# Layer 0 of a four-layer convolution stack: loads written into the expansion, last product with two pixel rows as column tiles

## The chip, the core and the metric

The kernel runs on one core of a Trainium2 chip. TensorE (PE) multiplies matrices out of SBUF into PSUM, VectorE (DVE) and ScalarE (ACT) work on SBUF and PSUM, GpSimd (POOL) and SyncE (SP) mostly issue DMAs here. The metric is the time of one execution on the device in microseconds (us), lower is better; of several runs the median is taken.

## The reference

The input x has 4 images of 64 channels and 256 x 256 pixels. Four layers follow each other, each of the form x = x + conv(group_norm(x)). Only the first matters here:

```python
def _L0_conv_ref(x, w_in, w_dw, fft_filter, w_out):          # hidden = 192, c2 = 384
    x = jnp.einsum('bchw,oc->bohw', x, w_in)                 # 64 -> 384 channels
    # 8 x 8 patches: filter each patch in the frequency domain
    xf = jnp.fft.rfft2(xp) * fft_filter
    xp = jnp.fft.irfft2(xf, s=(8, 8))
    # depthwise 3 x 3 convolution over the whole image
    x = lax.conv_general_dilated(x, w_dw, (1, 1), [(1, 1), (1, 1)], feature_group_count=384)
    x1, x2 = jnp.split(x, 2, axis=1)
    x = jax.nn.gelu(x1, approximate=False) * x2
    return jnp.einsum('bchw,oc->bohw', x, w_out)             # 192 -> 64 channels

x = x + _L0_conv_ref(_gn(x), ...)                            # 32 groups of 2 channels
```

The three layers behind it (a 3 x 3 convolution, a masked one, and a Fourier layer) are not touched.

## The kernel before

All arithmetic is in float32. Layer 0 treats the filter in a patch and the 3 x 3 convolution as one linear map from the 64 pixels of a patch (and its neighbours to the right and below) to 64 pixels, with matrices for each of the 384 channels that are made once at the start (`tables`, `weights`) and kept in DRAM (`wts`).

An image has 32 rows of 32 patches. Eleven rows form a block, three blocks an image, twelve blocks in all (`blocks`; p counts them, i0 is the first patch row, -1, 10 or 21). A block is worked in four quarters (kb) of 48 of the 192 channel pairs. A quarter has two stages:

- The expansion (`expand`, lines 444 and 450 on PE): for each of up to 12 patch rows t, the normalized input is multiplied by `w_in` into PSUM, with pixels on partitions. Even t take 32 PE instructions of 128 columns of weights, odd t 64 of 64 columns. ACT and DVE each copy half of the result into the tile u (line 459 for even t, lines 461 to 463 for odd t). Two rows t are in PSUM at once.
- The convolutions (`convolve`, lines 494 and 503 on PE), g = 0 to 11: four channel pairs each. ACT takes the GELU (line 510), DVE multiplies (line 511), and POOL stores the tile h to the DRAM tensor g of the block (line 514). The weights w come from `wts` by SP (line 471), one load for two g.

The last product of layer 0, 192 to 64 channels by `w_out`, needs all four quarters of a block. So it runs one block late: block p - 1 is projected while block p is worked, in 16 units, one after each of the convolutions g = 1, 4, 7 and 10. A unit (`project`) covers one pixel row r of the patches (8 of them) and four of the eight pixel columns (half 0 or 1). Its g loads (`load_g`, lines 546 and 550) and the x rows for the residual (`load_r`, line 559) come by SP. Of the 192 channels 128 are multiplied with `wo1` (line 591), 64 with `wo6` (line 598). The two column tiles of PE are the left and the right half of the image row (s). A unit works on two banks of PSUM, and each instruction covers the valid patch rows only: 11 rows give 176 columns, 10 rows 160. The DVE adds the product to the residual tile r (lines 607, 610, 612); after the second half it takes bn_stats of r for the next layer's norm (line 618), and POOL stores r (line 622). The units of the last block run alone at the end.

The loop also loads x for the next image's statistics (`load_stats`, line 627, summed by DVE in line 320) and, in the fourth quarter, the rows of the next block (`load_x`, line 418, normalized by ACT in line 256).

The order on PE, DVE, ACT and SP is the order of the program, written by hand; only POOL's is left to the framework. An engine waits for nothing but semaphores: buffers that come free, and data. So SP works off its DMA list as fast as buffers allow. PSUM is four pairs of banks, taken in turn. The rings of SBUF buffers are `l0x` 4 (x and statistics), `l0w` 4, `l0h` 4, and 2 each for the g loads and r.

## Time and profile before

| | us |
|---|---|
| median of 3 runs | 6649.44 |
| lowest, highest | 6638.31, 6666.61 |
| profiled execution | 6626.21 |
| its span in the profile | 6624.4 |
| mean granted PE clock in it | 0.953 |
| first projection unit, last one (start) | 432.0, 4060.1 |

The numbers of the prediction come from the one profiled execution. Busy times of the engines overlap; what counts is which of them the others wait for in each stage. In a group's line the last part is the idle time of the engine just before these instructions, and what ended it: "<-ACT u L459" is a wait for ACT's line 459, "issue" a stop for which the profile shows no wait. PEld is the weight load of PE. A float32 matmul of the program is two instructions on PE.

### The profile page before, as it was taken

How to read it: one execution, taken by the hardware profiler on the slowest of the kernel's cores; microseconds unless marked ns; L12 is line 12 of the kernel's file. 1: busy time of each engine (PE TensorE's matmuls, PEld its weight loads, DVE VectorE, ACT ScalarE, POOL GpSimd, SP SyncE). 2: the span in 40 equal slices, each digit the busy share in tenths (PEclk: the TensorE clock that was granted, in tenths of full speed). 3: DMA queues.
4: the chain of work that ended last, by engine and by line, in shares of the span. 5: the costliest groups of instructions: out<-in, count | busy, mean ns of one | idle time of the engine just before them, and what ended most of it. 6: DMA issues, size and time to landing. Idle time of an engine off the chain costs nothing.

```text
span 6624.4 us, 238282 instructions
## 1 busy us (share of the span) xinstructions
PE 6040.5 (91%) x106712; PEld 3213.7 (49%) x106712; DVE 4275.7 (65%) x5924; ACT 3238.8 (49%) x4564; POOL 1050.4 (16%) x1646
## 2 busy tenths in 40 slices
PE   2999999999999999999999986999899999999987
PEld 1455555555555555555555543333344444443576
DVE  5556555555555555555555545999798898885355
ACT  4454434344434444344444422777777887783211
POOL 3111111111111111111111111111022222221011
PEclk9999999999999999999999997999999999999855
DMA  8577777777878877877767669999666666677889
GB/s 236 152 206 211 216 213 222 218 216 213 230 213 238 219 222 207 223 214 220 210 193 206 188 194 247 232 229 228 165 177 176 168 180 173 173 187 264 318 351 394
DMA packets 878510, 1447.67 MB, mean 219 GB/s; under 512 B 77252, under 2 KB 586452, under 8 KB 875444
## 3 DMA queue, kind: packets, MB, share of 16 engines
q1 hardware_dynamic: 725284, 923.09, 54.8%
q0 software_dynamic: 148672, 500.14, 21.7%
q8 instruction: 843, 13.81, 0.9%
q10 hardware_dynamic: 3536, 9.20, 0.5%
q14 instruction: 175, 1.43, 0.1%
HBM read 932.08 MB, written 500.04 MB: 216 GB/s over the span
## 4 chain that ended last, share of the span: by engine, by line
PE 82%; DMA 6%; ACT 5%; DVE 3%; issue 3%; SPq 0%; POOL 0%; ACTq 0%; DVEq 0%; POOLq 0%
PE pc L503 18%; PE pc L494 12%; PE m L869 10%; PE psu L444 9%; PE one L1110 8%; PE div L1069 6%; PE po L591 4%; ACT u L459 4%; PE psu L450 4%; PE psz L1099 2%; PE po L598 2%; DMA x<-x 2%; PE psa L1297 2%; DMA g<-g 2%; PE psy L1444 1%
## 5 line engine op out<-in xcount | busy, mean ns | idle before, releaser
L511 DVE TENSOR_TENSOR h<-h,pc 128x374 f32<-128x374 f32 x1152 | 574.7, 541 | 1268.7 <-ACT h L510 1267.7
L510 ACT ACTIVATE h<-pc 128x374 f32<-128x374 f32 x1152 | 492.6, 480 | 1824.9 <-PE pc L503 1822.0
L503 PE MATMUL pc<-u,w 64*16 64x374 f32 (+2 forms) x27648 | 1244.1, 483 | 0.0
L494 PE MATMUL pc<-u,w 64*64 64x374 f32 x9216 | 928.6, 494 | 81.1 <-DVE u L463 32.2
L514 POOL DMA_DIRECT2D g<-h x576 | 416.7, 723 | 3111.0 <-DVE h L511 2904.7
L503 PEld LDWEIGHTS pc<-u,w 64*16 64x16 f32 (+2 forms) x27648 | 413.8, 92 | 769.5 <-issue 768.9
L444 PE MATMUL psu<-win,xn 64*128 64x96 f32 x8704 | 627.0, 283 | 131.8 <-ACT u L459 110.5
L459 DVE COPY u<-psu 64x384 f32<-64x384 f32 x1088 | 604.3, 555 | 167.7 <-PE psu L444 155.7
L459 ACT COPY u<-psu 64x384 f32<-64x384 f32 x1088 | 560.0, 515 | 238.9 <-PE psu L444 218.8
L444 PEld LDWEIGHTS psu<-win,xn 64*128 64x128 f32 x8704 | 574.0, 192 | 202.6 <-ACT u L459 143.6
L1055 DVE TENSOR_TENSOR q<-xn 128x2313 f32<-128x2313 f32 (+2 forms) x256 | 627.4, 2492 | 1.7 <-ACT xn L256 1.7
L1110 PE MATMUL one<-z,wp 32*32 32x512 f32 x16384 | 592.1, 596 | 17.8 <-issue 13.6
L494 PEld LDWEIGHTS pc<-u,w 64*64 64x64 f32 x9216 | 350.3, 133 | 531.0 <-issue 354.7
L256 ACT ACTIVATE xn<-x,nb,r 128x1024 f32<-128x1024 f32 (+3 forms) x272 | 486.8, 1793 | 244.6 <-DMA x<-x 140.8
L1056 ACT ACTIVATE q<-q 128x2313 f32<-128x2313 f32 (+2 forms) x256 | 529.0, 2086 | 32.7 <-DVE q L1055 31.2
L450 PE MATMUL psu<-win,xn 64*64 64x96 f32 x17408 | 458.2, 252 | 81.9 <-issue 57.2
L1069 PE MATMUL div<-q,ones 64*32 64x512 f32 x8192 | 466.3, 594 | 12.9 <-ACT q L1056 9.3
L1110 PEld LDWEIGHTS one<-z,wp 32*32 32x32 f32 x16384 | 367.6, 103 | 223.6 <-issue 80.1
L450 PEld LDWEIGHTS psu<-win,xn 64*64 64x64 f32 x17408 | 395.5, 137 | 126.0 <-issue 77.0
L1143 POOL DMA_DIRECT2D x<-r x512 | 275.5, 547 | 969.8 <-DVE r L1140 945.1
L591 PE MATMUL po<-g,wo 128*64 128x176 f32 (+1 forms) x3072 | 315.8, 348 | 63.3 <-DMA g<-g 41.3
L869 PE MATMUL m<-t,wk 64*64 64x512 f32 x3072 | 341.1, 588 | 0.0
(162 smaller groups left out, 6668.1 us busy)
## 6 DMA issues: line engine op xcount, KB each, us to landing
g<-h POOLq DMA_DIRECT2D x576, 374.0 KB, 7.0
x<-x SPq DMA_DIRECT2D x240, 640.0 KB, 6.4
w<-wt SPq DMA_DIRECT2D x288, 448.0 KB, 8.4
x<-x SPq DMA_DIRECT2D x100, 1024.0 KB, 14.2
g<-g SPq DMA_DIRECT2D x414, 187.0 KB, 5.7
g<-g SPq DMA_DIRECT2D x736, 93.5 KB, 6.0
x<-in_x_dram SPq DMA_DIRECT2D x256, 256.0 KB, 8.1
x<-o POOLq DMA_DIRECT2D x128, 512.0 KB, 8.2
```

Source lines behind the costliest of these rows:

```text
L444: nc.tensor.matmul(ps[s][:, k, at], xn[halves[s], n : n + 2].rearrange("p n r w -> p (n r w)"), win[halves[s], kb, 0 : 2 * PB], start=True ...
L450: nc.tensor.matmul(ps[s][halves[1 - odd], k, at], xn[halves[s], n + odd].rearrange("p r w -> p (r w)"), win[halves[s], kb, PB * (1 - odd) ...
L459: copy(at(h, 8 * s + o), v[k, c : c + PB])
L494: nc.tensor.matmul(out(C * c, C, k, h), w[halves[h], k, 2 * (G % 2) + c, 0:C], cells(h, 4 * g + 2 * k + c, 0, 0), start=True, stop=False, ...
L503: nc.tensor.matmul(out(q, m, k, h), w[halves[h], k, 2 * (G % 2) + c, c0 : c0 + m], cells(h, 4 * g + 2 * k + c, down, right), start=False, ...
L511: nc.vector.tensor_mul(h[:, k], h[:, k], ps[k][:, 1, 0:L])
L591: nc.tensor.matmul(out(k, s, x), wo1, moving(g1[:, 2 * k], 2 * half + k, s, x), start=(x == 0), stop=False, skip_group_check=True,)
L869: nc.tensor.matmul(rows2(m)[halves[j], s], w[dx][halves[s]], ts[n][halves[s], i, 2 * j : 2 * j + 2, dx : dx + W], start=(dx == 0), stop=(d ...
L1055: nc.vector.tensor_sub(d, p0, p1)
L1056: nc.scalar.activation(d, d, AF.Square)
L1069: ins = nc.tensor.matmul(ps[quarters[j], h], ones[halves[h]], q[n, g, k][halves[h], r + 2 * j : r + 2 * j + 2, o : o + W], start=(m == 0), ...
L1110: ins = nc.tensor.matmul(rows2(ps[g])[quarters[j], k], w[quarters[i]], z[quarters[i], h, 2 * j + dy : 2 * j + dy + 2, dx : dx + W], tile_p ...
```

## The change

- A unit now covers two pixel rows and two of the eight pixel columns: n // 4 gives the pair of rows, n % 4 the pair of columns. The two column tiles of PE are the two pixel rows. Each instruction takes all 374 columns of a plane as it lies in memory, halo and invalid rows too, so a unit has 8 matmuls of 374 columns instead of 16 of up to 176. DVE then picks the valid elements out of PSUM with two adds of 352 elements (four where the two rows have different limits).
- The residual tile holds two pixel rows at full width, in two buffers as before: loads and stores of r move runs of 1 KB, where they moved 512 bytes.
- The channels are assigned anew to `wo1` and `wo6`, and a unit's g loads are four DMAs (some split in two), by 96, 32, 64 and 64 partitions, in runs of 2 x 374 and 374 elements.
- The weights in DRAM lie so that a w load has one run of 3584 bytes on each partition, where it had two of 1792.
- The units stand after g = 0, 3, 6 and 9. The g loads of the units after g = 0 and 3 follow their unit at once; those of the units after 6 and 9 are kept in the list `later` and stand in the next expansion behind t = 7 and t = 9. The r load stands behind g = 1, for a block's first quarter in the expansion. Loads of x (statistics or next rows) stand in the expansion behind t = 9, 10 and 11, the others as before.
- The statistics of r are a list `tasks` of six bn_stats chunks for a row pair, filled by the fourth unit of a quarter (g = 9); two are taken after each convolution that has no unit, one behind each t of an expansion.
- The rings `l0x`, `l0w` and `l0h` have 3 buffers instead of 4, and the w load looks two ahead instead of three.

The diff, cut to its core:

```diff
-        p_xn, p_x = pool("l0xn", NR + 1), pool("l0x", 4)
-        p_w, p_h = pool("l0w", 4), pool("l0h", 4)
+        p_xn, p_x = pool("l0xn", NR + 1), pool("l0x", 3)
+        p_w, p_h = pool("l0w", 3), pool("l0h", 3)
...
-        wts = [dr.tile([2, 64, 2, Q, NC], F32, name=f"wt{t}") for t in range(HID // C)]
+        wts = [dr.tile([2, 64, Q, 2, NC], F32, name=f"wt{t}") for t in range(HID // C)]
...
+        def load_g(p, n):
+            if not (0 <= p < NB and n < 16):
+                return
+            rr, q0 = (2 * (n // 4), 2 * (n // 4) + 1), 2 * (n % 4)
...
+            g1 = pools[0].tile([128, 2, 2 * L], F32, tag="g1", name=f"g1_{p}_{n}")
+            g6 = pools[1].tile([128, 2, L], F32, tag="g6", name=f"g6_{p}_{n}")
+            loads[p, n] = g1, g6
+            parts = [(g1[Q:128], 1, slice(0, HID // 2), q0, 2), (g1[0:Q], 0, slice(C, HID // 2), q0, 2)]
+            parts += [(g6[halves[q]], 0, slice(0, C), q0 + q, 1) for q in range(2)]
...
+        def split(lo, hi):
+            out = [(k, min(2, hi - k)) for k in range(lo, hi, 2)]
+            if len(out) < (NR + 1) // 2:
+                out[-1:] = [(hi - 2, 1), (hi - 1, 1)]
+            return out
...
+            for q in range(2):
+                for s in range(2):
+                    nc.tensor.matmul(
+                        po[halves[s], q, 0:L], wo1, g1[:, s, q * L : (q + 1) * L],
+                        start=True, stop=False, skip_group_check=True,
+                    )
+            for q in range(2):
+                for s in range(2):
+                    nc.tensor.matmul(
+                        po[halves[s], q, 0:L], wo6[halves[q]], g6[halves[q], s],
+                        start=False, stop=True, tile_position=(q * C, s * C), skip_group_check=True,
+                    )
...
+                    o = rt[h, lo:hi].rearrange("p i (j x w) -> p w i x j", x=2, w=P)[:, (q0 + q + 1) % P]
+                    nc.vector.tensor_add(o, o, v)
...
+            def stats(at, chunks):
+                for h, (i, m) in chunks:
+                    nc.vector.bn_stats(bst[h, at, :], rt[h, i : i + m].rearrange("p i w -> p (i w)"))
+            chunks = zip(*([(h, c) for c in split(lo, hi)] for h, lo, hi in groups))
+            tasks.extend((stats, next(slot), c) for c in chunks)
...
+        def task(n=1):
+            for _ in range(min(n, len(tasks))):
+                f, *args = tasks.pop(0)
+                f(*args)
...
                     for t in range(NR + 1):
                         if 0 <= i0 + t < NP:
                             expand(p, kb, t)
+                        task()
+                        if t in (7, 9) and later:
+                            load_g(*later.pop(0))
+                        if t == 7 and kb == 0:
+                            load_r(p - 1, 0)
+                        if t >= 9:
+                            if kb == 3 and t - 9 < len(fresh):
+                                load_x(fresh[t - 9])
+                            elif kb < 3 and nk:
+                                loaded.append(nk.pop(0))
+                                load_stats(b + 1, loaded[-1])
                     for g in range(NG):
                         G = NG * kb + g
                         if g % 2 == 0:
-                            load_w(p * (HID // 8) + G // 2 + 3)
+                            load_w(p * (HID // 8) + G // 2 + 2)
                         convolve(p, kb, g)
                         if g < NG - 1:
                             self.next_norms()
-                        if g in (1, 4, 7, 10):
-                            unit()
+                        if g in (0, 3, 6, 9):
+                            unit(wait=g > 3)
+                        else:
+                            task(2)
+                        if g == 1 and kb < 3:
+                            load_r(p - 1, kb + 1)
```

## The prediction

> **What bounds the kernel now.** I read the page first, then a table of four stretches of one quarter block of layer 0, then the groups of instructions inside layer 0's blocks, then two stretches of the timeline. The page gives the engine shares and the DMA by slices:

> ```profile
> span 6624.4 us, 238282 instructions
> PE 6040.5 (91%) x106712; PEld 3213.7 (49%) x106712; DVE 4275.7 (65%) x5924; ACT 3238.8 (49%) x4564; POOL 1050.4 (16%) x1646
> DMA  8577777777878877877767669999666666677889
> ```

> TensorE (PE) is busy nine tenths of the span, and the change touches only layer 0 (slices 3 to 25, about 390 to 4062 us). DMA at 0.7 to 0.8 there is an average over two very different stages. The table by stretches shows them for one expansion (1121 to 1147) and the convolutions after it (columns: busy us of each engine, granted clock, DMA share, GB/s):

> ```profile
> 1121.00:1135.00 14.00, 11.72 (x312) 10.72 (x305) 10.85 (x21) 10.02 (x20) 0.96 (x2) 1.00 1.04 299
> 1135.00:1147.00 12.00, 8.59 (x248) 7.71 (x240) 9.35 (x18) 8.73 (x18) 0.00 (x0) 1.00 0.08 16
> 1150.00:1200.00 50.00, 50.00 (x880) 21.23 (x882) 24.66 (x41) 9.41 (x22) 10.42 (x14) 1.00 0.87 249
> ```

> In the convolutions PE never stops and VectorE (DVE) works half the time. In the expansion PE has gaps, DVE works almost all the time, and the DMA is full for 14 us and then idle for 12. The groups say why PE stops in the expansions of all blocks (390 to 3940 us; the last part is PE's idle time and what ended it):

> ```profile
> L444 PE MATMUL psu<-win,xn 64*128 64x96 f32 x8064 | 578.7, 282 | 123.1 <-ACT u L459 101.8 <-issue 18.7 <-ACT u L462 2.0
> L450 PE MATMUL psu<-win,xn 64*64 64x96 f32 x15872 | 418.0, 252 | 57.5 <-issue 57.2
> ```

> So 102 us go to copies out of PSUM, and 18.7 + 57.2 = 75.9 us to "issue", where no wait explains the stop. Around these stops the instruction queue's 16 KB fetches are in flight and come late, so I take them for late instructions. The timeline of an undisturbed expansion shows the copy loop:

> ```profile
> 3701.93 2.03 PE L444 MATMUL psu<-win,xn 64*128 64x96 f32 x32
> 3702.57 1.00 DVE L511 TENSOR_TENSOR h<-h,pc 128x374 f32<-128x374 f32 x2 [0.55 <-ACT h L510]
> 3704.03 2.26 DVE L459 COPY u<-psu 64x384 f32<-64x384 f32 x4 [0.47 <-PE psu L444]
> 3706.24 2.20 PE L444 MATMUL psu<-win,xn 64*128 64x96 f32 x32 [0.80 <-ACT u L459]
> 3708.47 2.26 DVE L459 COPY u<-psu 64x384 f32<-64x384 f32 x4 [0.45 <-PE psu L444]
> 3709.31 2.19 SPq L559 DMA_DIRECT2D r<-in_x_dram  x2
> ```

> Even rows' copies (2.26 us on DVE) free the PSUM pair, PE then needs 2.2 us for the next even row, and only then can DVE go on: a ring of 4.44 us for two rows (3704.03 to 3708.47). DVE idles 0.45 us in each turn, but a delay of DVE larger than that is never made good. The last line matters too: SP issues an r load at 3709 that stands in the program behind a convolution and a unit beginning after 3728. SP runs ahead of PE as far as buffers allow.

> **The projection units (PE).** A unit now is 12 steps: 16 wo1 matmul instructions two at a time, 16 of wo6 four at a time, 176 columns each:

> ```profile
> 1011.43 1.60 PE L591 MATMUL po<-g,wo 128*64 128x176 f32 x16
> 1012.95 0.92 PE L598 MATMUL po<-g,wo 64*64 64x176 f32 x16
> 1013.68 0.50 PE L494 MATMUL pc<-u,w 64*64 64x374 f32 x2
> ```

> That is 1013.68 − 1011.43 = 2.25 us; with ten patch rows (160 columns) about 2.05. The new unit has half the instructions, always 374 columns: 4 + 2 = 6 steps. A convolution has 10 steps of 374 columns (16 instructions four at a time, 48 eight at a time) in 3.52 us, 0.352 a step with its switches, so 6 × 0.352 = 2.11 us. Ends: 6 × 0.31 = 1.86 (spacing of the steps of L494 alone), or 2.25 / 2 × 374 / 176 = 2.39 if time goes strictly by column. I take 2.11, whose row has these very columns. Of the 176 units beside convolutions 114 have eleven rows, 62 ten: 114 × 0.14 − 62 × 0.06 = 12 us saved (56 saved to 37 lost).

> **Statistics moved into DVE's ring.** The residual adds stay 352 elements for each pixel column, and lie beside convolutions, where DVE has half its time free: nothing, as before. The bn_stats are as many as before (six chunks a row pair, 0.64 us each at 512 elements, 0.40 at 256), but leave their place. Their row in the view of that line (shortest, median, longest ns):

> ```profile
> L618 DVE BATCH_NORM_STATS2 bst<-r x288: 404/676/699, 448.4 to 4064.2; 128x6 f32<-128x512 f32 x96, 128x6 f32<-128x384 f32 x32, 128x6 f32<-128x256 f32 x16
> ```

> Two of 512 in a row take 1.28 us in the timeline, hence 0.64. Before, three follow a unit inside the convolutions. Now six are queued at g = 9 and drain two at g = 10 (free), two behind the last convolution, one behind expansion row 0, one behind row 1. Waiting behind them on DVE are the copies, and behind those PE. With X the start of the expansion: DVE ends the last products at X + 1.64 (3703.57). Even first row, before: copies of row 2 begin at 3708.47, X + 6.54. After: 1.64 + 1.28 = 2.92; copies 2.26, 5.18; a chunk 0.64, 5.82; odd copies 1.70, 7.52; a short chunk 0.40, 7.92. Delay 1.38. By the same steps: both late chunks short (ten-row blocks), 1.14; odd first row, where three chunks stand ahead of the first copies, 5.66 against 3.75 (1042.75 to 1046.50 in the timeline), 1.91; seven expansions behind a pair whose two rows have unequal limits, where every chunk is two instructions, 3.46. Twelve each of the first three: 16.6 + 13.7 + 22.9 + 7 × 3.46 = 77 us on the path. Ends: 0, if PE would be stopped there by late instructions anyway, and 43 × 2.6 = 112, if nothing of it finds a gap. I take 77, from the undisturbed rows.

> **The loads.** Writing two of four g loads of a quarter and three image loads into expansion rows 7 to 11 moves them in SP's program, not in time: their buffers are free from g = 7 to 9 on, and the last thing SP waits for ahead of them is the w load of g = 10. So they go out about 9 us ahead of the expansion (only in a block's first quarter do they wait for the last g store). That is 2 × 1.15 + 3 × 0.52 = 3.9 MB, with stores and w some 5.5 MB, 18 to 22 us at 249 to 299 GB/s: the DMA is full until about X + 12, where it now is until X + 14. The r load, which now runs ahead into the expansion, no longer does, as it stands behind a g load that waits for its unit. Instruction stops: in the timelines some 13 of the 75.9 us lie in the first 8 us of expansions, where DVE will be late anyway, and 45 past 14 us, some 18 of these in second and third quarters, where the DMA will be quiet sooner. I take 13 + 9 = 22 saved, ends 76 saved and 40 lost. [...]

> **Shallower rings.** h, 4 to 3: from ACT's start to landing 1.8 + 7.1 (median of the blocks; longest 10.7), 12.5 at worst; three convolutions and a unit are 12.7: nothing, though little is left. w, 4 to 3: the load at g = 4 stands behind unit 1's g load, which waits for PE; 4 × 3.52 + 2.1 − 4.1 of issue = 12.1 us are left for a landing of 8.6 (longest 13.3; the 4.1 are SP's for a unit's g loads from 1016.22 on). x, 4 to 3: ScalarE's normalization has 11 us for 8.1 to 11.5, and some 2 us of slack behind it. I put 3 us (0 to 25).

> **The tail** (3937 to 4062, last block's units alone) is bound by DMA, share 1.04 to 1.07. r moves 5.8 of its 29 MB, now in 1 KB runs where there were 512 B, and half of it before the first g store has landed. Against that stand four adds and twelve statistics for the last, unequal pair, some 6 us. Net 6 saved (15 saved to 6 lost). [...]

> **Sum.** −12 + 77 − 22 + 3 − 6 = +40 us. The profiled execution took 6626.2 us (span 6624.4), below the median of three by 23; 6626.2 + 40 = 6666, and on the median 6649.4 + 40 = 6689. Its own range is +5 to +80.

> **Rivals.** (1) Stalls overlap: PE stops for DVE instead of for instructions, and the 77 swallow the 76. Then −12 + 1 − 6 + 3: about −14, no change. For it: both are about 1.75 us an expansion; against it: most stops lie late, past the first two rows. (2) Faster: the DMA is quiet through all expansions, the 75.9 us vanish, the steps cost 1.86, and half of DVE's delay finds gaps: −56 − 76 + 38 − 6 = −100; with the steps at 2.11, −56. It needs SP's burst not to come, and decides once the stops fall under some 20 us. (3) Slower still: w is late. If its landing behind a g load passes 12.1 us, PE waits at g = 8 in each quarter: 1.5 us × 44 = 66, together +106; the longest landings now (13.3) are past that point. (4) The wide units are no cheaper (2.39) with all else as forecast: +89.

> **Numbers.** Forecast 0.5, rival 1 0.2, rival 2 0.12, rivals 3 and 4 together 0.18. About 0.5% (33 us) is what a measurement can tell from no change. Of the forecast's half, 0.31 lies above +33; with 0.18, slower is 0.49. Faster: 0.12 and 0.03 of rival 1, 0.15. Same: 0.36. The range goes from −50 (6600) to +115 (6765); the likeliest case alone has 6654 to 6729.

> **What would show it.** Right: units of 2.1 us; two bn_stats of r behind the last product and one each between the first copies, with the even copies of row 2 at X + 7.9; expansions longer by 1 to 2 us, the idle time of L444 ended by DVE copies up by some 70; SP's g issues ahead of X. Wrong: no bn_stats ahead of the copies, issue stops in the expansions at zero or above 100 us, PE waiting for w or h.

## The result, and the profile after

The changed kernel takes 6832.19 us (median of 4 runs, 6830.44 to 6843.61), the kernel before 6643.88 us in the same comparison (6630.05 to 6666.61). The ratio is 1.028, with a 95% interval of 1.0254 to 1.0306: slower by 2.8%, some 186 us. The forecast was +40 us with a range that ended at +115; the sign was right, the size was not, and the time lies above the range.

The page of the changed kernel, the lines that were shown of before:

```profile
span 6828.7 us, 230801 instructions
PE 6112.8 (90%) x103640; PEld 3120.7 (46%) x103640; DVE 4339.7 (64%) x6132; ACT 3242.0 (47%) x4564; POOL 975.4 (14%) x1550
DMA  8476778677878786867676769999956667667889
```

PE executes 3072 instructions fewer and is busy 72 us longer (6112.8 against 6040.5), at a mean granted clock of 0.936 in place of 0.953. The groups of PE inside layer 0's blocks (390 to 4270 us) say where:

```profile
L445 PE MATMUL psu<-win,xn 64*128 64x96 f32 x8064 | 616.0, 294 | 160.1 <-ACT u L460 101.3 <-DVE u L460 31.8 <-issue 23.6
L451 PE MATMUL psu<-win,xn 64*64 64x96 f32 x15872 | 458.3, 264 | 104.8 <-issue 75.5 <-ACT u L464 18.4 <-DVE u L464 6.4
L495 PE MATMUL pc<-u,w 64*64 64x374 f32 x8496 | 861.3, 495 | 107.6 <-DVE u L460 27.8 <-DVE u L464 27.5 <-DMA w<-wt 27.0
```

These are the same expansion instructions as L444 and L450 before, in the same number. Before, they were busy 578.7 + 418.0 = 996.7 us and had 123.1 + 57.5 = 180.6 us of idle time ahead of them; now 1074.3 and 264.9. That is +78 us of busy time and +84 us of waiting, +162 us together. Stops taken for late instructions ("issue") went from 75.9 to 99.1, where 22 us less were forecast. Waits for w (27.0 us) are new in the convolutions; the view of before has none.

The whole difference of the spans, 204 us, by stages (sums over PE's stretches in the two traces): expansions +162, of which 121 in the blocks' first quarters (291.5 to 412.1); convolutions +44; units beside them −21; from the last convolution to the last product of layer 0 −14 (124.2 to 110.3); the first block +8; from the last product to the end of the program +26; the start −1.

The table by stretches shows a typical expansion, the one that the prediction showed for before (block 3, second quarter), and the convolutions behind it:

```profile
1183.70:1197.70 14.00, 11.11 (x284) 10.01 (x276) 12.47 (x23) 9.58 (x19) 0.71 (x1) 1.00 1.03 336
1197.70:1213.30 15.60, 12.33 (x269) 11.37 (x269) 9.79 (x18) 9.29 (x19) 0.00 (x0) 0.78 0.18 46
1215.00:1265.00 50.00, 47.78 (x749) 17.25 (x757) 20.73 (x37) 8.56 (x20) 7.83 (x11) 0.97 0.76 210
```

The loads stand in rows 7 to 11, but the DMA is full in the first 14 us (share 1.03) and nearly idle in the second half (0.18): as forecast, SP issued them early. The timeline shows it, and what comes of it:

```profile
1175.20 5.27 SPq L553 DMA_DIRECT2D g<-g  x8
1181.81 9.09 SPq L633 DMA_DIRECT2D st<-in_x_dram  x6
1183.69 1.55 PE L451 MATMUL psu<-win,xn 64*64 64x96 f32 x64
1185.26 1.87 DVE L618 BATCH_NORM_STATS2 bst<-r 128x6 f32<-128x512 f32 x3
1199.56 1.60 PE L445 MATMUL psu<-win,xn 64*128 64x96 f32 x12 [2.30 <-issue]
1201.09 2.84 PE L451 MATMUL psu<-win,xn 64*64 64x96 f32 x64
1203.85 2.87 PE L445 MATMUL psu<-win,xn 64*128 64x96 f32 x32
1206.65 1.55 PE L451 MATMUL psu<-win,xn 64*64 64x96 f32 x64
```

The g loads go out 8.5 us ahead of the expansion (1183.69), as in each of the 33 expansions that are not a block's first. The statistics stand among the first copies, as forecast. Then at 1199.56 PE has stood still for 2.30 us with no wait that explains it, and behind that stop the next rows take 2.84 and 2.87 us, where 1.55 and 2.0 to 2.3 are usual: the granted clock is 0.50 for 6.83 us from 1198.82 on (0.78 in the mean of this stretch). **This second payment is what the forecast had no term for.** From the first expansion of block 1 to the last convolution the time at half clock grew from 123 to 328 us. It comes in pieces of 3.41 us and multiples of it. The +78 us of busy time above are its direct price in the expansions.

That such a stop is a wait for instructions is inferred from the packets of the instruction queue (q8 on the page). The expansions of blocks 1 to 11 have 30 issue stops over 1.5 us, and in each a 16 KB packet of that queue lands 1.3 to 1.7 us before PE goes on (here at 1197.86). The DMA's share was 0.83 or more in the 8 us before each of the 30 stops; during four of them it was already down to 0.1 or less. A full DMA alone is not enough, though: in the convolutions shown for before it has a share of 0.87, and PE never stops.

First quarters are the worst. In the blocks with eleven new rows (p = 1, 3, 4, 6, 7, 9, 10) the last of these rows is now loaded so late that ScalarE waits for it at the end of the fourth quarter, and ScalarE's copies of the next expansion stand behind it. One piece of the chain of waits from 1060 to 1110 us (start, us, what), and the timeline there:

```profile
1082.36 15.48 DMA x<-in_x_dram
```

```profile
1097.92 1.24 ACT L256 ACTIVATE xn<-x,nb,r 128x1024 f32<-128x1024 f32 x1 [6.88 <-DMA x<-in_x_dram]
1100.68 2.94 PE L451 MATMUL psu<-win,xn 64*64 64x96 f32 x64 [6.90 <-ACT u L464]
1103.55 3.73 PE L445 MATMUL psu<-win,xn 64*128 64x96 f32 x32
1107.21 2.84 PE L451 MATMUL psu<-win,xn 64*64 64x96 f32 x64
1107.43 11.82 SPq L633 DMA_DIRECT2D st<-in_x_dram  x6
...
1126.95 1.43 PE L451 MATMUL psu<-win,xn 64*64 64x96 f32 x32 [3.71 <-issue]
```

The load takes 15.48 us, ScalarE idles 6.88 us, PE 6.90 us, and then works at half clock (3.73 us for a row of 2.0 to 2.2). Moreover SP has been held by the last g store of the block, and then sends two g loads, r and three statistics loads (six DMAs) one behind the other, from 1100.26 to 1119.25 (the SPq line is the last of these); PE's next instructions come 3.71 us late, at 1126.95. Stops of 3.1 to 4.7 us like this one lie in the first quarters of nine of the eleven blocks. This expansion took 38.1 us; in the second quarter of the block it was 29.6.

Last, behind the final product of layer 0:

```profile
4229.34 1.43 SPq L565 DMA_DIRECT2D r<-in_x_dram  x2
4238.37 0.86 PE L588 MATMUL po<-g,wo 64*64 64x374 f32 x8 [0.29 <-DMA g<-g]
4243.71 0.73 DVE L606 TENSOR_TENSOR r<-r,po 64x352 f32<-64x352 f32 x1 [12.09 <-DMA r<-in_x_dram]
4250.65 8.82 DVE L606 TENSOR_TENSOR r<-r,po 64x352 f32<-64x352 f32 x12
4259.51 7.60 DVE L618 BATCH_NORM_STATS2 bst<-r 64x6 f32<-64x512 f32 x12
4269.81 0.56 PE L203 MATMUL gn<-mv,sb_c_avg 128*128 128x1 f32 x2 [30.58 <-DVE mv L200]
```

PE's products are done at 4239.2, but the last r load was issued at 4229.34 and is waited for until 4247.46. Adds and statistics of a row pair with unequal limits follow one by one, and layer 1's norm begins 30.58 us after the last product. Before, this took 5.64 us:

```profile
4066.98 0.56 PE L203 MATMUL gn<-mv,sb_c_avg 128*128 128x1 f32 x2 [5.64 <-DVE mv L200]
```

### The profile page after: what moved, and what is told of

It reads as the page before. It is cut to its first block, busy times and chain, and to the rows that moved or that the text cites. A ratio compares the mean times of both kernels' runs of the same rounds, so it can differ in the third digit from the quotient of the medians.

```text
span 6828.7 us, 230801 instructions
## 1 busy us (share of the span) xinstructions
PE 6112.8 (90%) x103640; PEld 3120.7 (46%) x103640; DVE 4339.7 (64%) x6132; ACT 3242.0 (47%) x4564; POOL 975.4 (14%) x1550
## 4 chain that ended last, share of the span: by engine, by line
PE 71%; DMA 13%; DVE 8%; ACT 3%; issue 3%; SPq 1%; POOL 0%; ACTq 0%; DVEq 0%; POOLq 0%
PE pc L504 14%; PE pc L495 10%; PE m L893 10%; PE one L1134 8%; PE psu L445 7%; PE div L1093 6%; DMA w<-wt 4%; PE psu L451 3%; PE po L582 3%; DVE u L460 3%; DMA x<-in_x_dram 2%; DMA x<-x 2%; ACT u L460 2%; PE psz L1123 2%; DMA g<-g 2%
## 5 line engine op out<-in xcount | busy, mean ns | idle before, releaser
L511 ACT ACTIVATE h<-pc 128x374 f32<-128x374 f32 x1152 | 492.7, 480 | 1812.8 <-PE pc L504 1784.3
L445 PE MATMUL psu<-win,xn 64*128 64x96 f32 x8704 | 663.4, 294 | 167.9 <-ACT u L460 109.0
L445 PEld LDWEIGHTS psu<-win,xn 64*128 64x128 f32 x8704 | 603.7, 203 | 246.3 <-ACT u L460 140.7
L451 PE MATMUL psu<-win,xn 64*64 64x96 f32 x17408 | 500.2, 264 | 135.2 <-issue 79.1
L451 PEld LDWEIGHTS psu<-win,xn 64*64 64x64 f32 x17408 | 433.3, 146 | 181.5 <-issue 103.9
L606 DVE TENSOR_TENSOR r<-r,po 128x352 f32<-128x352 f32 (+3 forms) x448 | 317.7, 741 | 208.0 <-PE po L588 169.0
L582 PE MATMUL po<-g,wo 128*64 128x374 f32 x1536 | 295.3, 504 | 54.3 <-DMA g<-g 54.0
```

What stands on the lines that cost most here:

```text
L445: nc.tensor.matmul(ps[s][:, k, at], xn[halves[s], n : n + 2].rearrange("p n r w -> p (n r w)"), win[halves[s], kb, 0 : 2 * PB], start=True ...
L451: nc.tensor.matmul(ps[s][halves[1 - odd], k, at], xn[halves[s], n + odd].rearrange("p r w -> p (r w)"), win[halves[s], kb, PB * (1 - odd) ...
L582: nc.tensor.matmul(po[halves[s], q, 0:L], wo1, g1[:, s, q * L : (q + 1) * L], start=True, stop=False, skip_group_check=True,)
```

## Experiments

Each row of the table is one kernel. "us" is (ratio − 1) × 6644, so that all are against the kernel before; the half-widths of the intervals are 10 to 25 us. The next columns are from the profiled execution of each: busy and idle time of the two expansion groups of PE, the "issue" part of that idle time, PE's waits for w in the convolutions (– where the view has none), and the length of the four convolution stages over blocks 1 to 11. This last column holds the wait ahead of the last block's first unit too (12.7 us before, 27.0 in the changed kernel), which the list by stages counts with the last block. The expectation of a_paced counts the changed kernel's stops in another way (137 us); the table takes the groups' view (75.9 before, 99.1 after).

| kernel | ratio, interval | us | exp. busy | idle | issue | w | conv. |
|---|---|---|---|---|---|---|---|
| before | 1 | 0 | 997 | 181 | 76 | – | 1964 |
| changed | 1.028, 1.0254–1.0306 | +186 | 1074 | 265 | 99 | 27 | 2022 |
| a_stats_conv | 1.0235, 1.0204–1.0267 | +156 | 1061 | 250 | 114 | 26 | 2023 |
| a_loads_conv | 1.0176, 1.0139–1.0214 | +117 | 1046 | 211 | 39 | 47 | 2046 |
| a_both_conv | 1.0141, 1.011–1.0172 | +94 | 1030 | 205 | 58 | 43 | 2042 |
| b_rings3 | 1.0091, 1.006–1.0122 | +60 | 1005 | 185 | 75 | 39 | 2027 |
| b_x3 | 1.0045, 1.0029–1.0062 | +30 | 996 | 182 | 57 | – | 2004 |
| b_w3 | 1.0077, 1.005–1.0105 | +51 | 1002 | 171 | 63 | 46 | 2030 |
| p_rings4 | 1.0231, 1.0216–1.0246 | +153 | 1093 | 266 | 161 | – | 1977 |
| a_rings4 | 1.0409, 1.0389–1.0428 | +272 | 1154 | 322 | 196 | – | 1996 |
| a_norm_later | 1.0224, 1.0209–1.0239 | +149 | 1072 | 234 | 91 | 18 | 2019 |
| a_both_norm | 1.0114, 1.0076–1.0152 | +76 | 1007 | 191 | 56 | 47 | 2052 |
| a_paced | 1.0422, 1.04–1.0444 | +280 | 1010 | 183 | 10 | 200 | 2263 |
| a_paced_w | 1.0317, 1.0294–1.0339 | +211 | 1026 | 197 | 27 | 134 | 2177 |
| a_paced_best | 1.0288, 1.0256–1.0319 | +191 | 1004 | 182 | 46 | 145 | 2196 |
| b_paced | 0.9926, 0.9904–0.9949 | −49 | 968 | 140 | 6 | – | 1984 |

**a_stats_conv: the statistics back inside the convolutions.** The six chunks are issued at g = 9 (three) and g = 10 (the rest), nothing in an expansion.

```diff
-                        task()
                         if t in (7, 9) and later:
...
                             unit(wait=g > 3)
-                        else:
-                            task(2)
+                        if g == 9:
+                            task(3)
+                        if g == 10:
+                            task(len(tasks))
```

> The changed kernel, but the six statistics chunks of a row pair are drained inside the convolutions (three behind the unit of g = 9, the rest behind g = 10), none in the expansion. Before took about 6644 us, the changed kernel 6832. Theory A, statistics in VectorE's copy ring are the main cost (the forecast's 77 us, more where stops also halve PE's clock): 6700 to 6750, 80 to 130 less than the changed kernel, and the first quarters' expansions fall by several us each. Theory B, the late last x load of a block behind a ring of three: 6770 to 6800, since only the forecast's own 40 to 60 us go, and seven first-quarter expansions keep ScalarE's wait of about 7 us. Theory C, the burst of loads in the expansions: 6770 to 6800 likewise, and the instruction stops of the first quarters stay.

30 us are regained, which is the outcome of theories B and C. The expansions' copies are waited for 47 us less, but the issue stops rise from 99 to 114, as if part of DVE's delay had lain over stops that are now paid by themselves.

**a_loads_conv: the loads back where they stood.** g follows its unit at once, r stands at the block's start, statistics loads stand at g % 3 == 0, the first three rows of x at the end of the third quarter.

```diff
-                        if t in (7, 9) and later:
-                            load_g(*later.pop(0))
...
-                            unit(wait=g > 3)
+                            unit()
...
+                            if kb == 2 and g == NG - 1:
+                                for row in fresh[:3]:
+                                    load_x(row)
```

> The changed kernel, but its loads stand where they were: each unit's next g load right behind it, the first two g loads and the first r load at the start of a block, image loads for the statistics at every third g, and the next block's first three rows behind the last convolution of the third quarter. Rings stay at three, statistics stay in the expansion. Theory C (loads written into the expansion make bursts that delay instructions, w and x): 6700 to 6750. Theory B (ring of three for x): no better than 6790, the wait of ScalarE at the end of a block stays. Theory A: 6800 to 6830.

69 us are regained, and the issue stops fall from 99 to 39 us. So the new places of the loads, which were forecast to save 22 us, cost 69. The time (6761) lies next to theory C's range.

**a_both_conv: both undone.** What stays is the new projection with its residual, the w layout and the rings of three.

> The changed kernel with both undone, statistics inside the convolutions and loads where they were; what is left is the new projection, the wider r and w runs and the rings of three. Theories A and C together: 6610 to 6650, at or under the kernel before. Theory B: 6710 to 6750, as the ring of three still makes the last x late and PE then runs at half clock.

+94 us stay, in theory B's range. With a_loads_conv this makes a ladder, a row of kernels each of which has one more part of the change: statistics 117 − 94 = 23 us beside loads at their old place, loads 186 − 117 = 69. In the other order the statistics are 186 − 156 = 30 and the loads 156 − 94 = 62.

**b_rings3: the kernel before with the three rings at 3.** Nothing else is changed but the look-ahead that follows from it (w two ahead, x three).

```diff
-        p_xn, p_x = pool("l0xn", NR + 1), pool("l0x", 4)
-        p_w, p_h = pool("l0w", 4), pool("l0h", 4)
+        p_xn, p_x = pool("l0xn", NR + 1), pool("l0x", 3)
+        p_w, p_h = pool("l0w", 3), pool("l0h", 3)
...
-                            load_w(p * (HID // 8) + G // 2 + 3)
+                            load_w(p * (HID // 8) + G // 2 + 2)
```

> The kernel before with the rings of x, w and h at three instead of four and the w load two ahead, x rows three ahead; nothing else of the change. Theory B: 6720 to 6760 (seven blocks with about 7 us of wait and as much again of half clock, and w late at some g): ScalarE waits for the last x rows of a block. Theories A and C: 6640 to 6665, no more than 20 us above the kernel before.

+60 us from the rings alone, for which the forecast had 3 (0 to 25); theory B expected more still (6720 to 6760), A and C at most 20. Two single rings tell which, first x, then w (each by its own lines of the diff above):

> The kernel before with only the x ring at three and rows loaded three ahead; b_rings3 with all three rings took 6704 against 6639. If x makes b_rings3's loss (its fourth quarters, +78 us of expansions and convolutions): 6685 to 6705. If w does: 6640 to 6660.

> The kernel before with only the ring of w at 3 (loaded two ahead instead of three). The three rings at 3 cost 60 us, that of x alone 23. If w is the rest: 6665 to 6685 beside 6641, with PE waiting for w some 30 us in all. If h is the rest, or the rings only cost together: 6640 to 6655.

x alone costs 30 us, w alone 51; both times (6663 and 6701) miss the expected ranges. The group of PE's waits in b_w3, and where they lie: the fourth quarters' convolutions grew from 503 to 567 us, the others by about 5 at most.

```profile
PE pc L494 <- DMA w<-wt: 46.4, 11, 5.3
```

Eleven waits, one a block, up to 5.3 us. They lie at g = 10. In the fourth quarter SP has the next block's rows of x in its list, each waiting for a buffer that ScalarE's normalization frees; w stands behind them, and with one load less ahead of time this shows. The prediction looked at the queue in front of w only for g loads. 30 + 51 is more than 60, though with intervals of 11 to 21 us that the two waits cover each other is only likely. In the changed kernel w is waited for elsewhere: at g = 6 of first and second quarters (22 us), where its load stands behind g and r loads, and at g = 8 of fourth quarters (4 us).

**p_rings4 and a_rings4: rings of four, paid for with one r buffer.** In both the r ring has one buffer, which makes the room, and its load stands behind g = 11; p_rings4 does so to a_both_conv, a_rings4 to the changed kernel.

```diff
-            p_r = pool("l0r", 2, side="right")
+            p_r = pool("l0r", 1, side="right")
...
-                        if g == 1 and kb < 3:
+                        if g == NG - 1 and kb < 3:
                             load_r(p - 1, kb + 1)
```

> The projection by two pixel rows alone: statistics and loads as in a_both_conv, and the rings of x, w and h at four again with the old look-ahead. To make room r has one buffer, and its load stands behind g = 11. Before about 6640 us, a_both_conv 6734. If the shallower rings are what is left in a_both_conv (theory B): 6600 to 6650, since the units are shorter (20 us less in PE's units) and the last block's end some 10. If the new g loads or the wide units cost by themselves: 6690 or more.

> The changed kernel as it is, loads and statistics in the expansion, but with rings of four for x, w and h, the old look-ahead, and one buffer of r, loaded behind g = 11. Changed kernel 6832. Theory B (rings): 6700 to 6740, first-quarter expansions 5 to 7 us shorter, no waits of PE for w. Theory C (bursts of loads): 6780 or more, since the instruction stops of the first quarters stay.

Both are slower, by 59 and 86 us, outside every expected range but the open ones ("6690 or more", "6780 or more"). The convolutions go back to 1977 and 1996 us and PE no longer waits for w, which fits the rings as what lengthened them. But the r load has to wait for the store of the same buffer, in SP's waits for a_rings4:

```profile
SPq L565 <- DMA x<-r: 465.0, 33, 16.0
```

SP stands still for 16.0 us at worst and then sends everything at the start of the expansion; issue stops rise to 161 and 196 us. The busy time of the expansion's instructions rises with them, to 1093 and 1154, and the mean granted clock of the profiled execution falls: 0.935 in place of 0.945 in a_both_conv, 0.924 in place of 0.936 in the changed kernel.

**a_norm_later: the late row off ScalarE's path.** The eleventh new row is normalized behind t = 5 of the next expansion.

```diff
                             k = g - 1
+                            if k == 10:
+                                pending.append(fresh[k])
+                                continue
                             normalize_x(fresh[k])
...
                             expand(p, kb, t)
+                        if t == 5 and pending:
+                            normalize_x(pending.pop())
```

> The changed kernel, but the eleventh new row of a block, which is normalized behind g = 11 of the last quarter and whose load is late there, is normalized behind row 5 of the next expansion, so that ScalarE's copies are not queued behind that wait. Theory B, ScalarE's wait of 7 us in seven blocks with the half clock that follows: 6740 to 6780. If the wait only hides another (theory C, the g loads of the first quarter and the late instructions): 6810 to 6830.

37 us less, and the first quarters' expansions fall from 412 to 372 us. The late row is shown as a cause; it is a third of what the first quarters lost. The gain lies in four of the seven blocks (p = 1, 3, 6, 9: 8 to 11 us each); in the other three ScalarE's wait for the row is gone too, but PE's busy time rises by up to 4 us and the expansion is at most 2 us shorter.

**a_both_norm: the same edit in a_both_conv.**

> Statistics and loads as in the kernel before (a_both_conv), and besides the eleventh new row of a block is normalized behind t = 5 of the next expansion. My theory: ScalarE's wait for that row, PE's stop behind it and the half clock after the stop are costs of their own, beside those of the loads and the statistics; then the gains add, 98 + 47 = 145 us below the changed kernel: 6687, within 15, first quarters' expansions about 325 us in place of 367, half-clock time down to some 150 us. Rival: stops stand in for one another (with one gone, the next late instruction or copy takes its place); then at most half of the 47 is seen, 6710 to 6735.

+76 in place of +94, with intervals that overlap: the median (6730) lies in the rival's range, but the four runs go from 6709 to 6754, and whether the gains add can't be told from the times. By the profile the first quarters' expansions fell from 367 to 338 us and the half-clock time from 218 to 157 us, while the convolutions grew by 10 us.

**a_paced: the loads held to the place where they are written.** Each load of g, x or statistics that stands in an expansion waits for a copy of ScalarE from the row it stands behind: by the code the last of the row's copies on ScalarE, where the expectation says the first. The r load has no such wait; it is held by the g load ahead of it on SP. (The calls of `dma_start` in `load_g`, `load_x` and `load_stats` are wrapped in `paced`.)

```diff
+        def paced(d):
+            if pace:
+                self.after(d, pace[-1])
...
-                            expand(p, kb, t)
+                            pace[:] = [expand(p, kb, t)]
```

> The changed kernel, but each load that is written into an expansion (g behind t = 7 and 9, r, statistics, rows of x) waits for ScalarE's first copy of the row it stands behind, so that SP cannot issue it ahead of its place. Theory A: the loads harm because SP issues them about 9 us ahead of the expansion, and their burst makes instructions late in its first half; held to their place they go out when the DMA is idle: issue stops in the expansions 137 -> 80 to 100, the time 6770 to 6800. Theory B: any transfer beside an expansion makes instructions late, wherever in it; then the stops only move to the second half, and the time stays at 6820 to 6850.

```profile
L450 PE MATMUL psu<-win,xn 64*128 64x96 f32 x8064 | 598.1, 283 | 163.2 <-ACT u L466 118.3 <-DVE u L466 34.5 <-DVE bst L626 7.1
L456 PE MATMUL psu<-win,xn 64*64 64x96 f32 x15872 | 412.0, 250 | 20.2 <-DVE u L471 9.9 <-issue 8.5
L503 PE MATMUL pc<-u,w 64*64 64x374 f32 x8472 | 888.3, 510 | 282.2 <-DMA w<-wt 200.3 <-DVE u L466 27.7 <-DVE u L471 27.5
```

The two expansion groups first: issue stops are down to 10 us (8.5 and a rest), and the expansions are 146 us shorter. So A named the cause of the stops rightly: the burst at the place where SP sends it, ahead of the expansion or into its first half. Yet the time is 94 us above the changed kernel's, which neither theory had: the convolutions wait 200.3 us for w, whose loads stand behind the held ones on SP (first quarters 99 us, nearly all at g = 6). The early burst had also been a head start.

**a_paced_w: the first w load of a quarter put ahead of the held loads.**

```diff
                 for kb in range(4):
+                    load_w(p * (HID // 8) + NG * kb // 2 + 2)
                     for t in range(NR + 1):
...
-                        if g % 2 == 0:
+                        if g % 2 == 0 and g > 0:
```

> The changed kernel with its expansion loads held to their place (as in a_paced), and the w load that stood behind them put ahead of the expansion. My theory: order on SP's queue. a_paced lost its 144 us of gain in the expansions because w stood behind paced loads; with w ahead PE's 200 us of waits for w fall below 50, and the time is 6740 to 6800, below the changed kernel's 6832. Rival: the DMA cannot carry the loads in the shorter time whatever their order; then the waits stay above 100 us, now for g and h as well, and the time is over 6850.

The waits for w fall only to 134 us, and the time is +211, in the rival's range. Moving this load is worth 69 us. But the rival's reason, that no order would do, is not shown: the load that was moved is that for g = 4, while 86 of the 134 us lie at g = 6 of first quarters, whose load still stands at g = 2 behind the held loads. In the first quarter of block 2 the trace has its buffer free at 779 us (end of g = 1), SP issues it at 794.2, behind a g, an r and a statistics load, and PE waits for it from 796 to 808.8. Whether that load, put ahead too, would be in time was not tried. a_paced_best adds the statistics in the convolutions and the late row:

> a_paced_w with the statistics inside the convolutions (g = 9 and 10) and the eleventh new row normalized behind t = 5 of the next expansion. If the costs of DVE's ring and of the late row are their own: another 60 to 80 us below a_paced_w, 6670 to 6730. Rival: as in a_both_norm one stall takes the place of another: within 25 us of a_paced_w.

+191, 20 us below a_paced_w and within its interval's reach, the rival's outcome: again stalls stand in for one another (idle time in the expansions falls by 15 us, waits for w rise by 11).

**b_paced: the kernel before with its loads held.** Rings of four, old projection and statistics; g and r for a block's first units, the g load of the unit after g = 10 (and with it what stands behind it) and the first four rows of x are written into rows 7 to 11 and wait for the row's copy.

```diff
-                            unit()
+                            unit(g == 10)
...
+                        if t in (7, 9) and later:
+                            load_half(*later.pop(0))
+                        if kb == 3 and t >= 8 and t - 8 < len(fresh):
+                            load_x(fresh[t - 8])
```

> The kernel before (rings of four, its own projection and statistics), with the loads that SP issues ahead of an expansion held to rows 7 to 11: g and r of a block's first units, the g load of the unit after g = 10 and with it all that stands behind it, and the first four rows of x. Theory A: late instructions come from that burst; issue stops 76 -> under 25 us, half-clock time 123 -> under 70, the expansions 50 to 80 us shorter, time 6560 to 6600. Theory B: the burst is needed where it is, since what is held back then collides with w and g in the first convolutions; the expansions gain, the convolutions lose as much or more: 6640 to 6750.

```profile
L450 PE MATMUL psu<-win,xn 64*128 64x96 f32 x8064 | 576.8, 279 | 130.7 <-ACT u L466 128.7 <-DVE u L466 1.0 <-DVE h L520 0.8
L456 PE MATMUL psu<-win,xn 64*64 64x96 f32 x15872 | 390.7, 247 | 8.9 <-issue 6.0 <-ACT u L471 2.6
```

6599.43 us, ratio 0.9926 (0.9904 to 0.9949): theory A's range, 0.7% faster than the kernel before and 3.4% faster than the changed one. Issue stops are 6.0 us in place of 75.9, half-clock time 79 in place of 123 (under 70 was expected), the expansions 70 us shorter in busy and idle time; ScalarE's copies take 27 us of the freed time, and the convolutions give back 20 us. So the idea behind the loads' new place holds, if they really go out there. Here w is three loads ahead and PE never waits for it; that this is what a_paced_w lacked is likely, but was not tested by itself, as the projection, the statistics and the other rings differ too.

## Why the prediction was wrong

**What held.** PE's units: the new one takes 2.09 us (1080.98 to 1083.07 in the timeline, forecast 2.11), and they gained 21 us beside the convolutions (forecast 12). SP's early issue was foreseen (8.5 us ahead, about 9 said), and so was the DMA's full first half. The statistics stand in DVE's ring as drawn; their delay showed in PE's waits for DVE's copies (31.8 us now, under 1 before), and undoing them brought 30 us with the loads moved and 23 without, against 77 in the sum.

**The term that failed first: the loads, −22.** It was +69. Two steps of it were wrong. "the DMA is full until about X + 12, where it now is until X + 14" was taken to end stops sooner; in the stretch shown the DMA was full for 14 us as before and a stop came at X + 13.6. And first quarters were put aside in a bracket ("only in a block's first quarter do they wait for the last g store"). That very wait gathers two g loads, r and three statistics loads into one burst, and the stops of 3.1 to 4.7 us follow. What the runs showed in place of 22 us saved, the changed kernel against a_loads_conv: 60 us more of issue stops (99 against 39), 28 us more of busy time in the expansions, 24 us less in the convolutions, and 69 us in all by the ratios. Most packets of the instruction queue bring no such stop: in the changed kernel 59 issue stops of the expansions stand beside 483 of its packets in the same stretch (390 to 4270 us). Still, the kernels that do not hold their loads have 39 to 196 us of such stops.

**The second: the shallower rings, 3 us.** They cost 60 us in the kernel before. What they cost in the changed kernel no run shows by itself, as p_rings4 and a_rings4 changed r's ring too. For x, "some 2 us of slack" was worked out with landings of 8.1 to 11.5 us; but in the changed kernel the same transfers land later, in the list of DMA issues (bytes, then median us from issue to landing):

```profile
x<-in_x_dram SPq DMA_DIRECT2D x216, 256.0 KB, 10.3
st<-in_x_dram SPq DMA_DIRECT2D x172, 256.0 KB, 11.8
```

Before:

```profile
x<-in_x_dram SPq DMA_DIRECT2D x212, 256.0 KB, 8.1
st<-in_x_dram SPq DMA_DIRECT2D x172, 256.0 KB, 7.9
```

A slack of 2 us was spent by that alone, and single x loads land after up to 15.8 us. For w the wait behind g loads was looked at and put at nothing (12.1 us left for 8.6); in the changed kernel it is 22 us. The wait behind x rows in the fourth quarter, the main one in b_w3, was not looked at.

**The third: a stop was priced at its own length.** Half clock behind it was in no term, and at a granted clock of 0.50 rows took 2.84 and 3.73 us in place of 1.55 and 2.0 to 2.2. The half clock is nearly half of the expansions' loss (78 of 162 us). The kernels of the table put it at about one for one: from before to a_rings4 the idle time ahead of the expansion's instructions grew by 141 us and their busy time by 157, to the changed kernel by 84 and 78, to b_paced by −41 and −29. The stops themselves were often shorter than the 3.41 us of a piece at half clock: the one of 2.30 us that ended at 1199.56 came with 6.83 us at half clock. In the clock's records of both kernels the pieces start on a fixed grid of 3.41 us, and half clock went with PE's idle time in one window of the grid, all stops added. Of the windows at full clock in blocks 1 to 11 of the changed kernel, none of 882 with less than 1 us of idle time was followed by half clock, 23 of 80 with 1 to 1.75 us, and 32 of 33 with more. In the kernel before it is 0 of 922, 17 of 68 and 10 of 11.

**The tail, −6.** What precedes the last product gained 14 us (net 6, with some 6 against it, makes 12 in the sum); what follows lost 25. The "some 6 us" for four adds and twelve statistics left out that the r load of that pair is issued 10 us before the last product, behind g loads, lands 18 us later, and that the twelve adds and twelve statistics then run with nothing beside them (8.82 + 7.60 us).

**The rivals.** The third, "w is late", had its wait and the reason for it (27 us in 23 pieces, up to 3.1), but not its price of 66, and the place only nearly: g = 6 of the first two quarters and g = 8 of the fourth, where it said g = 8 of each. None of them held the combination. The range was bounded by single unknowns, each at its end, with no end for landings that get later because the loads are rearranged.

**By the ladder** the 186 us are: rings 60, the new projection with residual and w layout 33, statistics 23, loads 69, each known to some 20 to 30 us and in this order of undoing. The 33 are, from b_rings3 to a_both_conv by stages: units −20, last block up to its last product −11, behind it +21, expansions +42 (first quarters +75, fourth quarters −24, the others −9), convolutions +1. Of the first quarters' loss in a_both_conv (367 us, 338 without the late row, against 292 in b_rings3) only the late row's part was settled. By the traces the first quarters there have 35 us more of busy time, 19 us more of issue stops and 20 us of waits for DVE's last products that were not there; why was not tested. r's load is 704 KB in the changed kernel, where it was 352.

## What to carry to other kernels

The place of a load in a program is not its time: read from the trace when the last wait ahead of it on its queue ends and what then goes out together, and if its time matters, hold it by a wait on the compute and move ahead of it what must not wait. Where PE's stops add up to more than 1 us, price half clock behind them: in the kernel before and the changed one it followed 42 of 44 windows of 3.41 us with over 1.75 us of idle time, and 40 of 148 with 1 to 1.75 us. A ring that gives up a buffer must be priced with the landing times of the new traffic and with everything that stands ahead of the load in its queue. When several small stalls compete, undo each alone and all together before adding them.
